# A perceiver layer on one core: the relative tables of self attention by column halves, and who makes four turning copies and two table copies

## The chip, the core and the metric

The kernel runs on one core of one Trainium2 chip. The core has a matrix engine (TensorE, PE in the profile, with PEld for its weight loads), VectorE (DVE), ScalarE (ACT), GpSimd (POOL) and SyncE (SP), which issues most transfers. The metric is the device time of one execution in microseconds (us). Before the change it is 780.18 us, the median of three runs from 779.72 to 780.61.

## What is computed

The layer has three parts, each added to its input: a cross attention of 128 positions to a context of 2048, a self attention with learned relative positions, and a gated attention that stands where a feed-forward block would. There are 4 sequences, 128 positions, width 512 and 16 heads of 32. All is in float32. The change is in the second part:

```python
r = jnp.arange(S)
rel = jnp.clip(r[:, None] - r[None, :], -MAX_DIST, MAX_DIST) + MAX_DIST
...
q, k, v = (proj(Wq), proj(Wk), proj(Wv))
a_q = Eq[rel]
a_k = Ek[rel]
a_v = Ev[rel]
content = jnp.einsum('bhld,bhmd->bhlm', q, k)
rel_k = jnp.einsum('bhld,lmd->bhlm', q, a_k)
rel_q = jnp.einsum('bhmd,lmd->bhlm', k, a_q)
pos_pos = jnp.einsum('lmd,lmd->lm', a_q, a_k)
logits = (content + rel_k + rel_q + pos_pos) * scale
attn = jax.nn.softmax(logits, axis=-1)
out = jnp.einsum('bhlm,bhmd->bhld', attn, v) + jnp.einsum('bhlm,lmd->bhld', attn, a_v)
```

For one position `l`, `rel_k` is the product of a window of the table (128 distances x 32) with the queries of that position in all 64 pairs of a sequence and a head. The kernel makes it so: 128 small products for `rel_k`, and 128 for `rel_q`.

## The kernel before

The cross attention takes the first three quarters of the time. It works through 16 blocks of 128 context positions in an order written out by hand. After it come the self attention (from about 600 us) and the gated attention (from about 695 us). In all three, each engine works through its instructions in the order in which the code issues them (`manual_schedule`), and waits on semaphores where a tile is not yet there or not yet free.

The stretch that the change touches stands at lines 799 to 887:

- `queries(c)` and `keys(c)`, for four chunks `c` of 128 columns: a projection on TensorE (`project_T`, line 215, 4 calls of 128x128 by 512) into a bank of the pool `bank`, and a copy to `qT` or `kT` by ACT (lines 868 and 873).
- `spread(src, n, half)`, after each second chunk: sixteen copies of 32x256 (line 811) that turn a part of `qT` or `kT` to the layout of `z`. In `z`, the four groups `g` of 32 partitions hold 32 positions each, and for each position the 64 pairs lie side by side. All of these "turning copies" are made by VectorE. `z[:, 0]` holds the queries, `z[:, 1]` the keys.
- `relative_k(n)` for `n` = 0 to 3, then `relative_q(n)` for `n` = 0 to 3: eight blocks. In each, `by_position` issues 32 matmuls (line 825), for eight positions and in turn for the four groups `g`. Each takes 32 rows of the table's window as weights, 128 columns wide, and 64 moving columns of `z`. Group `g` stands on its own 32 rows of the array and writes its own PSUM bank. A float32 matmul shows twice in the trace, with two weight loads.
- Blocks with even `n` write the four banks `psl` (tiles `s_rk`, `s_lg`), blocks with odd `n` two banks `pst` and two of the shared pool (tiles `s_rk` and `ps_rk`, `s_lg` and `ps_lg`). A block so waits for the copies of the block two before it, across the two tables.
- The first table's blocks are copied to `rk` (line 848): for `n` = 0 and 1 all four banks by ACT, for `n` = 2 and 3 banks 0 and 2 by ACT and 1 and 3 by VectorE.
- The second table's blocks go to `lg` with the positions' term `pos`: banks 0 and 2 by VectorE, which adds `pos` (line 863); banks 1 and 3 by ACT (line 860), and then GpSimd adds `pos` in SBUF (line 861). In the last block VectorE takes all four.

Then come the softmax's steps, again in an order by hand (lines 1065 to 1076): TensorE transposes parts of `rk` into PSUM (line 916) and adds the scores (line 931), VectorE joins them with `lg` (line 942) and takes maxima (line 948), ACT makes the exponentials (line 953). A join reads all positions of its heads, so it waits for all blocks and for GpSimd's additions. The tile `ev_win`, a load of 2 MB, takes the place of `z` and waits for the last product.

`by_columns` (lines 204 to 210) is an older helper, used in the cross attention: it issues one matmul as four, by 32 columns of the weights, each on its own column group.

## Time and profile before

| what | value |
|---|---|
| median of three runs | 780.18 us |
| the profiled execution, its time | 780.48 us |
| its span | 778.7 us |
| granted TensorE clock in it | 0.995 |
| the stretch 627.8 to 643.5 us: TensorE busy | 15.5 of 15.7 us |
| the same stretch: VectorE busy | 12.6 us |
| the same stretch: ACT busy | 10.7 us |
| the same stretch: GpSimd busy | 4.8 us |
| moved by DMA in it | 1 to 2% of the 16 engines' time |

The span runs from the first to the last instruction of one execution; the time of that execution is 1.8 us longer. The stretch is the one in which the eight blocks run. Its busy times are those of the profile's table by windows, two windows added. Further on, from 655 to 680 us, ACT is busy for 24.05 of 25 us with the exponentials.

In the profile a line such as `L825 PE MATMUL s_rk<-z,tabk 32*128 32x64` names the source line, the engine, the operation, the tile written and the tiles read, the weights' rows and columns, and the moving operand's partitions and columns. A helper's line stands for all of its callers.

### The profile page before, as it was taken

Reading aid. Unit: us, or ns where it says so; the run is one execution under the profiler, and the core shown is the slowest. Engines: PE = TensorE matmul, PEld = TensorE weight load, DVE = VectorE, ACT = ScalarE, POOL = GpSimd, SP = SyncE. Lnnn points to the kernel's source line nnn. Section 1 sums busy time; section 2 is a strip of 40 time slices with the busy share of each in tenths; the row PEclk is TensorE's granted clock in tenths of the full one; section 3 lists DMA queues with packets and bytes.
Section 4 is the critical chain, followed back from the end, with each engine's and each line's share of the span. In section 5 each row is a group of like instructions: output and inputs, shape, how many; then the busy total and the mean of one; then the engine's idle time right before and its main releaser. Section 6 shows DMA issues by size and latency. Waiting matters only on the chain.

```text
span 778.7 us, 28614 instructions
## 1 busy us (share of the span) xinstructions
PE 758.0 (97%) x13027; PEld 476.1 (61%) x13027; DVE 625.0 (80%) x642; ACT 527.6 (68%) x921; POOL 460.3 (59%) x296
## 2 busy tenths in 40 slices
PE   9999999999999999999999999997899999999998
PEld 5446566666666666666666666665253487674574
DVE  2158499999999999999999999998883689746463
ACT  2347777878788787887878878776813157923770
POOL 1623787859577595876958769599860015410261
PEclk9999999999999999999999999998999999999999
DMA  9310101101011010110101101033200005103001
GB/s 304 117 55 7 56 3 57 56 3 58 3 57 57 3 56 3 57 56 3 58 3 56 56 4 56 3 111 90 76 3 1 1 3 218 56 8 106 0 3 54
DMA packets 12619, 38.43 MB, mean 49 GB/s; under 512 B 1249, under 2 KB 1650, under 8 KB 10450
## 3 DMA queue, kind: packets, MB, share of 16 engines
q1 hardware_dynamic: 10802, 33.50, 12.5%
q8 instruction: 102, 1.67, 0.8%
q10 hardware_dynamic: 1248, 2.23, 0.8%
q0 software_dynamic: 448, 0.87, 0.5%
q14 instruction: 19, 0.16, 0.1%
HBM read 34.50 MB, written 2.10 MB: 47 GB/s over the span
## 4 chain that ended last, share of the span: by engine, by line
PE 88%; ACT 5%; DVE 5%; issue 1%; DMA 0%; POOL 0%; DVEq 0%; POOLq 0%; ACTq 0%
PE k L208 20%; PE ps_vu L208 12%; PE ps_s L458 9%; PE ps_vf L208 6%; PE ps_o L536 6%; PE ps_q L215 4%; PE ps_kc L208 3%; PE ps_vc L208 3%; PE ps_v L208 3%; ACT lg L953 2%; PE s_y L1367 2%; PE s_k L215 2%; PE out L208 2%; PE ps_k L215 2%; PE ps_k L556 2%; PE ps_sum L208 2%
## 5 line engine op out<-in xcount | busy, mean ns | idle before, releaser
L495 DVE TENSOR_TENSOR sg<-sg,stat 128x2048 f32<-128x2048 f32 x123 | 277.6, 2281 | 1.3 <-ACT rz L622 0.7
L470 ACT COPY sg<-ps_s 128x1024 f32<-128x1024 f32 x128 | 128.3, 1016 | 37.0 <-PE ps_s L458 21.5
L479 DVE TENSOR_TENSOR mx<-mx,ps_s 128x1024 f32<-128x1024 f32 x96 | 117.2, 1221 | 35.1 <-PE ps_s L458 22.6
L510 POOL TENSOR_TENSOR sm<-sm,sg 128x1024 f32<-128x1024 f32 x45 | 107.6, 2390 | 38.7 <-ACT sg L504 36.4
L504 ACT ACTIVATE sg<-sg 128x2048 f32<-128x2048 f32 x64 | 122.8, 1919 | 4.4 <-DVE sg L495 2.8
L511 POOL TENSOR_TENSOR sm<-sm,sg 128x1024 f32<-128x1024 f32 x45 | 107.5, 2389 | 3.5
L508 POOL TENSOR_TENSOR sm<-sg 128x1024 f32<-128x1024 f32 x16 | 38.4, 2398 | 93.8 <-ACT sg L504 93.8
L208 PE MATMUL k<-s,wk_sums 128*32 128x256 f32 x1440 | 86.7, 381 | 0.0
L458 PE MATMUL ps_s<-qT,kT 32*128 32x128 f32 x2048 | 76.8, 285 | 5.2 <-DVE mx L477 4.0
L458 PEld LDWEIGHTS ps_s<-qT,kT 32*128 32x128 f32 x2048 | 64.3, 188 | 24.6 <-issue 17.0
L208 PEld LDWEIGHTS k<-s,wk_sums 128*32 128x32 f32 x1440 | 43.9, 110 | 29.3 <-POOL s L311 0.2
L536 PE MATMUL ps_o<-sg,v 128*32 128x128 f32 x1792 | 60.1, 276 | 0.1
L536 PEld LDWEIGHTS ps_o<-sg,v 128*32 128x32 f32 x1792 | 51.9, 112 | 10.4 <-issue 1.3
L208 PE MATMUL ps_vu<-wv_sums,s 128*32 128x256 f32 x896 | 53.5, 379 | 0.0
L609 ACT COPY acc<-ps_o 128x512 f32<-128x512 f32 x56 | 32.9, 588 | 25.9 <-PE ps_o L536 24.7
L861 POOL TENSOR_TENSOR lg<-lg,pos 128x512 f32<-128x512 f32 x6 | 7.4, 1311 | 61.5 <-DVE lg L863 61.5
L208 PEld LDWEIGHTS ps_vu<-wv_sums,s 128*32 128x32 f32 x896 | 29.0, 110 | 19.2
L311 POOL TENSOR_TENSOR s<-ct,s 128x512 f32<-128x512 f32 x30 | 39.0, 1301 | 1.3
L311 POOL TENSOR_TENSOR s<-ct 128x512 f32<-128x512 f32 x30 | 38.6, 1287 | 0.2 <-PE ps_vu L208 0.2
L1265 POOL TENSOR_TENSOR e<-e,rs 128x512 f32<-128x512 f32 x16 | 16.3, 1040 | 36.6 <-DVE rs L1264 36.6
L606 ACT COPY ps_o<-acc 128x512 f32<-128x512 f32 x52 | 31.0, 596 | 6.4 <-DVE v L443 5.6
L489 DVE TENSOR_REDUCE stat<-mx 128x128 f32<-128x1024 f32 x16 | 32.8, 2052 | 0.1
(275 smaller groups left out, 1433.6 us busy)
## 6 DMA issues: line engine op xcount, KB each, us to landing
ct<-in_ctxT SPq DMA_DIRECT2D x15, 1024.0 KB, 4.8
ev_win<-in_tabv SPq DMA_DIRECT2D x1, 2048.0 KB
w_xattn_Wk<-in_xattn_Wk ACTq DMA_DIRECT2D x4, 256.0 KB, 6.5
ct<-in_ctxT SPq DMA_DIRECT2D x4, 256.0 KB, 6.4
x<-in_x SPq DMA_DIRECT2D x4, 256.0 KB, 8.6
w_xattn_Wv<-in_xattn_Wv ACTq DMA_DIRECT2D x1, 1024.0 KB, 12.4
w_xattn_Wq<-in_xattn_Wq SPq DMA_DIRECT2D x1, 1024.0 KB, 11.0
x_dram<-x SPq DMA_DIRECT2D x4, 256.0 KB, 2.4
```

The source lines that it names most:

```text
L208: nc.tensor.matmul(ps[cols], lhsT=lhsT[:, cols], rhs=rhs, start=start, stop=stop, skip_group_check=True)
L215: nc.tensor.matmul(ps, lhsT=w[:, k, c * P : (c + 1) * P], rhs=src[:, k, :], start=(k == 0), stop=(k == C - 1))
L311: nc.gpsimd.tensor_tensor(s_, x, y, op)
L458: nc.tensor.matmul(ps[i][:, cols], lhsT=kT[n, c // 2][rows, c % 2, cols], rhs=qT[rows, c, cols], start=(b == 0), stop=True, skip_group_che ...
L470: nc.scalar.copy(sg[n, c][:, k * HALF : (k + 1) * HALF], pss[n, c][k])
L479: nc.vector.tensor_tensor(mxs[n], mxs[n], pss[n, c][k], ALU.max)
L495: nc.vector.tensor_tensor(g, g, stat[:, row, :].unsqueeze(1).to_broadcast([P, NH * B, T]), op)
L504: nc.scalar.activation(sg[n, c], sg[n, c], AF.Exp, scale=SCALE)
L508: eng.tensor_tensor(t, g[:, 0:HALF], g[:, HALF:], ALU.add)
L510: eng.tensor_tensor(t, t, g[:, 0:HALF], ALU.add)
L511: eng.tensor_tensor(t, t, g[:, HALF:], ALU.add)
L536: nc.tensor.matmul(ps[i * HD : (i + 1) * HD, b * T : (b + 1) * T], lhsT=v[n, b // 2][:, b % 2, h * HD : (h + 1) * HD], rhs=sg[n, c][:, f * ...
```

## The change

A second helper issues a matmul as two, each with 64 columns of the weights, on its own half of the columns of the array and of the partitions of the PSUM bank. The tables' products use it: a block issues 64 matmuls instead of 32. Of the last group of turning copies (the keys' second half) those from the last 32 partitions of `kT`, one for each `g`, go to ACT. Of the first table's second block (`n` = 1), banks 1 and 3 are copied by VectorE instead of ACT.

```diff
+    def by_halves(ps, lhsT, rhs, start):
+
+        for i in range(2):
+            cols = slice(i * P // 2, (i + 1) * P // 2)
+            nc.tensor.matmul(ps[cols], lhsT=lhsT[:, cols], rhs=rhs, start=start, stop=True, skip_group_check=True)
...
-        def spread(src, n, half):
+        def spread(src, n, half, shared=False):
...
-                    nc.vector.tensor_copy(to[:, i, :, cs], from_[:, g])
+                    (nc.scalar.copy if shared and i == NH - 1 else nc.vector.tensor_copy)(to[:, i, :, cs], from_[:, g])
...
-                    nc.tensor.matmul(
-                        banks_of[g][:, j * NF : (j + 1) * NF],
-                        lhsT=tab[rows, s : s + T],
-                        rhs=z[rows, n, j0 + j, :],
-                        start=True,
-                        stop=True,
-                    )
+                    by_halves(banks_of[g][:, j * NF : (j + 1) * NF], tab[rows, s : s + T], z[rows, n, j0 + j, :], True)
...
-                copy = nc.vector.tensor_copy if n >= 2 and g % 2 else nc.scalar.copy
+                copy = nc.vector.tensor_copy if n >= 1 and g % 2 else nc.scalar.copy
...
             if c % 2:
-                spread(kT, 1, c // 2)
+                spread(kT, 1, c // 2, c == C - 1)
```

On TensorE, 256 matmuls of this stage become 512, so 512 entries of the trace become 1,024, with as many weight loads. On VectorE, 4 copies leave and 2 come. On ACT, 4 copies come, ahead of all copies of `rk`, and 2 leave. No transfer, no tile and no order between the engines' other instructions is changed.

## The prediction

> **What bounds the kernel now.** I read the page first, then the chain of waits for the stretch that the change touches, the rows by source line, and the timeline engine by engine.

> ```profile
> span 778.7 us, 28614 instructions
> PE 758.0 (97%) x13027; PEld 476.1 (61%) x13027; DVE 625.0 (80%) x642; ACT 527.6 (68%) x921; POOL 460.3 (59%) x296
> ```

> TensorE is busy for 97% of the span, but this average says little of one stage. The change touches only the relative tables, a stage of some 19 us, so the chain of waits (start, length, what) decides:

> ```profile
> 627.94 0.59 ACT kT L873
> 628.56 0.36 DVE z L811
> ...
> 634.37 0.38 DVE z L811
> 634.79 1.30 DVE rk L848 x2
> 636.13 1.90 PE s_lg L825 x59
> ...
> 643.49 1.90 PE s_l L916 x16
> ```

> Until 634.8 the end is set by VectorE's sixteen turning copies, then by two of its copies of the first table (`rk`), which free PSUM banks, and from 636 to 643.5 by the second table's products on TensorE (L825). So the stage has two limits in turn, and the diff touches both.

> What a product costs, by source line (least, median, greatest duration in ns):

> ```profile
> L825 PEld LDWEIGHTS s_rk<-z,tabk x192: 181/187/187, 627.8 to 635.4; 32*128 32x128 f32 x192
> L825 PE MATMUL s_rk<-z,tabk x192: 270/270/319, 627.8 to 635.5; 32*128 32x64 f32 x192
> ...
> L536 PEld LDWEIGHTS pso<-sg,v x128: 106/110/110, 571.1 to 582.9; 128*32 128x32 f32 x128
> L536 PE MATMUL pso<-sg,v x128: 272/273/297, 571.2 to 583.0; 128*32 128x128 f32 x128
> ```

> And the timeline (start, length, engine, line):

> ```profile
> 628.56 6.19 DVE L811 COPY z<-kT 32x256 f32<-32x256 f32 x16 [0.72 <-ACT kT L873]
> 634.79 1.89 DVE L848 COPY rk<-s_rk 128x512 f32<-128x512 f32 x3
> ...
> 629.91 3.03 ACT L848 COPY rk<-s_rk 128x512 f32<-128x512 f32 x6 [1.38 <-PE s_rk L825]
> ...
> 638.71 7.45 POOL L861 TENSOR_TENSOR lg<-lg,pos 128x512 f32<-128x512 f32 x6 [61.45 <-DVE lg L863]
> ...
> 629.89 0.28 PE L825 MATMUL s_rk<-z,tabk 32*128 32x64 f32 x2
> 629.91 0.28 PE L825 MATMUL ps_rk<-z,tabk 32*128 32x64 f32 x2
> 630.01 0.28 PE L825 MATMUL s_rk<-z,tabk 32*128 32x64 f32 x2
> ```

> A set of four (one per row group) starts within 0.02 us, and the next set comes 0.11 us later. GpSimd's six additions run without a gap from 638.71 to 646.16. The first join (L942) starts at 646.59, when the scores are done on TensorE.

> **The change, part by part.**

> *Products by halves.* Each of the 256 calls at L825 shows twice in the trace (two passes): 512 matmuls. A block is one relative_k or relative_q, 64 matmuls; 16 sets at 0.111 us make 1.78 us, and eight blocks 14.2 us. What is the 0.111? A load of 128 columns takes 187 ns and one of 32 takes 110, so a column costs 77/96 = 0.80 ns and 128 cost 103 ns: nearly the whole period. The 64 moving columns cost less: L208's rows of 256 and 512 columns (379 and 592 ns) give 0.83 ns a column, 53 ns. The set is bound by its weight load. A half loads 64 columns, 51 ns, so if two column groups load side by side a set of eight takes about 0.056 us, a block 0.9. Do they? L536 loads four column groups of 26 ns each. Loaded one behind the other, the first matmul after an idle stretch would lengthen by some 80 to 105 ns on the last group; the greatest there is 297 against a median of 273, +24. So they load side by side.

> What no row shows is the supply: twice as many pairs of load and matmul (1,024) at twice to four times the rate. Lower bound: four starts within 0.02 us, 7 ns a pair, eight in 56 ns, just enough. Upper bound: the fastest sustained row, L536, 32 in 0.88 us, 27.5 ns, so a block of 128 pairs takes 3.5 us. I take 7, because L536's 27.5 is explained by its own streaming (128 columns x 0.83 = 106 ns for four) and so says nothing of a limit on supply. The cost per block therefore lies between 0.9 and 3.5 us, taken 0.9; it is even with today's at 14 ns a pair.

> [...]

> *Four turning copies to ACT.* VectorE's last group shrinks from 16 to 12: 4 x 0.387 = 1.55 us, free at 633.2 instead of 634.75. ACT gets four copies of 32x256 ahead of its rk copies. No ACT row has this strided form. Its 128x512 PSUM copies follow each other at 0.49 us (six in 3.03, the last 0.58 long); an element costs (1016 - 588)/512 = 0.84 ns (L470 against L609), so 256 fewer make 0.28. The upper end is PE's strided row L1048 (four in about 0.15 us against L825's stream of 0.053), a factor 2.7: 0.75. I take 0.33, near the contiguous end: VectorE's copies of the same form follow each other at 0.387, little over half of the 0.6 of its 512-element copies, so the stride costs it little. ACT then ends its kT copy at 628.53, its turning copies at 629.85, and starts on block 0 when it does today (629.91), as the faster products have long arrived. At 0.75 it would finish 1.7 us later, at 633.6, about when VectorE becomes free; nothing is lost up to some 0.7 us a copy.

> *Half of block 1's rk copies to VectorE.* ACT loses two copies (0.98 us), VectorE gains two (1.2 us at 0.6). Behind them wait block 2's VectorE copies; for these wait the products of the second table.

> *The new order, step by step.* Blocks 0 and 1 on TensorE end at 628.7 and 629.6. ACT copies block 0 until 631.95; block 2 (same banks) runs until 632.9. VectorE ends turning at 633.2, copies two tiles of block 1 until 634.5 and two of block 2 until 635.7. Block 3 needs block 1's banks: 634.5 to 635.4. The second table's first block needs block 2's banks: 635.7 to 636.6. ACT's first lg copy ends at about 637.4 and GpSimd starts at 637.55, today 638.71: 1.2 us sooner. The remaining blocks alternate with copies (two a block on each engine, 1.25 us) and end at 640.2, 3 us sooner than today; transposes and scores end at 643.5 instead of 646.4.

> But the join needs GpSimd's additions too: 637.55 + 7.45 = 645.0. GpSimd takes TensorE's place as the last wait, 0.43 us of slack today. The join starts at 645.05 instead of 646.59: 1.5 us gained. Exponentials follow: ACT starts at 648.57 today, is nearly without gaps until 672, and moves along; it also loses its 0.2 us wait for the `v` copy at 655.17. Later weights (`ev_win`, ffn) start 3 us sooner, hidden either way. TensorE's 512 additional loads have no other place.

> **Sum.** 1.5 + 0.2 = 1.7 us off the span of 778.7: 777.0. The run profiled took 780.48, 1.8 above its span; the median of the three is 780.18. So 778.5. Within this likeliest case, 11 ns a pair (a block of 1.4 us) would give a gain of about 1.0, and GpSimd additions at the 1.04 us of L1265 in place of 1.24 would give 2.7: 777.5 to 779.2. What a measurement can tell from no change is 0.2%, 1.56 us; the bound is 778.62.

> **Rivals.**
> 1. *The product does not get faster* (the two halves of a row group load in turn, or supply is near 14 ns). Blocks stay at 1.8 to 1.9 us. VectorE is free sooner, but now has two copies more before block 3, at 634.5 instead of 634.0. Block 3 then ends at 636.3, the second table begins 0.3 us later and ends 0.2 to 0.5 later: 780.4. For it: no row has row and column groups together. Against it: L536's +24 ns.
> 2. *Supply of instructions, slower.* At 27.5 ns a pair a block takes 3.5 us, TensorE has no wait left, and eight blocks end at 627.84 + 28.2 = 656.0 instead of 643.4: 12.6 us later, 792.8. It decides from 14 ns a pair on; each ns above costs about 0.9 us. For it: no stretch of this trace sustains less than 27 ns. Against it: the fast starts, and that every such row is explained by its own columns.
> 3. *ACT's strided copies at 1 us or more.* Block 2 would start after 634.4, the second table at 637: the gain is eaten, 780.0 to 781.

> **Chances.** Forecast 0.62 (about three quarters of it beyond 0.2%), rival 1 0.17 (mostly no change), rival 2 0.15, rival 3 0.06 (half each). Faster 0.47, same 0.31, slower 0.22. The range 777.3 to 781.2 takes in the forecast, rivals 1 and 3; rival 2 and a little beside it lie outside.

> **What would show it.** After: loads of 64 columns at about 135 ns; a block's eight starts per 0.056 us, 16 such sets in 0.9 us; TensorE idle between the blocks; VectorE's last turning copies 12 in 4.7 us; GpSimd's additions starting near 637.5 and named as what released the first join. It is wrong if a block takes 1.8 us or more without waiting, if ACT's turning copies exceed 0.7 us, or if the joins begin sooner and the exponentials do not.

## The result and the profile after

The changed kernel takes 791.57 us, the median of four runs from 790.86 to 791.85; the kernel before takes 780.02 (four runs, 779.72 to 780.61). The ratio is 1.0144, with a 95% interval of 1.0132 to 1.0156: slower by 11.5 us, where 778.5 was forecast. The profiled execution took 790.86 us, its span is 789.1.

First the page, the engines and the row of the granted clock:

```profile
span 789.1 us, 29636 instructions
PE 760.1 (96%) x13539; PEld 477.1 (60%) x13539; DVE 625.2 (79%) x640; ACT 529.5 (67%) x923; POOL 460.8 (58%) x296
...
PEclk9999999999999999999999999998999959999999
```

TensorE is busy for 2.1 us more in a span that is 10.4 us longer: the rest is idle time. The 5 in the clock row is one slice of 20 us at about half clock. The rows by source line of the product (least, median, greatest ns) say that the tiles are as forecast where the clock is full, and that it isn't full for long:

```profile
L216 PEld LDWEIGHTS s_rk<-z,tabk x384: 127/131/227, 627.7 to 637.8; 32*64 32x64 f32 x192
...
L216 PEld LDWEIGHTS s_lg<-z,tabq x384: 173/222/228, 637.9 to 652.5; 32*64 32x64 f32 x192
```

A load of 64 columns takes 131 ns in the first table (forecast: about 135) and 222 in the second. The chain of waits through the second table:

```profile
630.98 2.06 ACT rk L848 x4
633.08 1.77 PE s_rk L216 x92
634.86 1.26 issue
...
638.37 1.22 issue
639.59 2.26 PE s_lg L216 x115
641.84 1.49 issue
...
645.58 1.49 issue
647.08 2.25 PE s_lg L216 x113
649.33 1.49 issue
```

After every run of matmuls TensorE stands still and waits for nothing that the profile shows ("issue"). Counted in the trace, these runs start at 636.12, 639.59, 643.33, 647.08 and 650.82, 3.47 to 3.75 us apart, and hold 128 pairs of load and matmul each (the last shows 121): 256 instructions. The queue that brings TensorE's instructions (q8) moves packets of 16 KB, 106 for the page's 27,078 matmuls and loads, 255 each. The change adds 1,024 instructions and 4 packets (102 to 106 in the whole execution), so a packet holds 256. From 627.6 to 653 it moved 7; before, 3 from 627.8 to 643.5 (packets, MB, share of the DMA engines' time):

```profile
q8 instruction: 7, 0.11, 1.9%
...
q8 instruction: 3, 0.05, 1.2%
```

A packet starts 1.04 to 1.14 us after each of these runs does (637.16, 640.69, 644.45, 648.22, 651.95), and the next run starts 2.4 to 2.6 us after the packet. My estimate from these times is a round trip, one packet at a time; what sets a packet off the trace doesn't show. The first two blocks, 256 pairs, ran from 627.65 to 630.44, 10.9 ns a pair.

The table by windows (window, its length, busy time of PE, PEld, DVE, ACT and POOL with their instructions, clock, DMA share, GB/s):

```profile
627.28:630.69 3.41, 3.38 (x258) 2.86 (x256) 2.62 (x7) 2.86 (x5) 0.00 (x0) 1.00 0.02 5
630.69:634.11 3.42, 2.02 (x110) 1.61 (x113) 3.31 (x8) 3.30 (x7) 0.00 (x0) 1.00 0.02 5
634.11:637.52 3.41, 2.15 (x144) 1.97 (x135) 1.50 (x3) 1.07 (x2) 0.00 (x0) 0.50 0.02 5
```

TensorE is busy for 2 of 3.4 us in the second window, and at its end the clock falls to 0.50; it comes back at 654.59. Two things are new, then: gaps in the supply and half a clock. The other engines wait for TensorE:

```profile
628.38 2.57 ACT L817 COPY z<-kT 32x256 f32<-32x256 f32 x4
...
642.42 2.49 POOL L861 TENSOR_TENSOR lg<-lg,pos 128x512 f32<-128x512 f32 x2 [65.30 <-DVE lg L863]
...
656.91 1.29 DVE L942 TENSOR_TENSOR lg<-s_l,lg 128x512 f32<-128x512 f32 x2 [1.54 <-PE s_l L931]
```

ACT's turning copies take 0.64 us each. GpSimd starts at 642.42 (before: 638.71), the joins at 656.91 (before: 646.59). These 10.3 us are, but for 0.1, the whole growth of the span.

### The profile page after: what moved, and what is told of

Read it like the earlier page. It is cut to its first block, busy times and chain, and to the rows that moved or that the text cites. A ratio compares the mean times of both kernels' runs of the same rounds, so it can differ in the third digit from the quotient of the medians.

```text
span 789.1 us, 29636 instructions
## 1 busy us (share of the span) xinstructions
PE 760.1 (96%) x13539; PEld 477.1 (60%) x13539; DVE 625.2 (79%) x640; ACT 529.5 (67%) x923; POOL 460.8 (58%) x296
## 4 chain that ended last, share of the span: by engine, by line
PE 88%; ACT 6%; DVE 4%; issue 2%; DMA 0%; POOL 0%; DVEq 0%; POOLq 0%; ACTq 0%
PE k L208 20%; PE ps_vu L208 11%; PE ps_s L464 9%; PE ps_vf L208 6%; PE ps_o L542 6%; PE ps_q L221 4%; PE ps_kc L208 3%; PE ps_vc L208 3%; PE ps_v L208 3%; ACT lg L953 2%; PE s_y L1367 2%; PE s_k L221 2%; PE out L208 2%; PE ps_k L221 2%; PE ps_k L562 2%
## 5 line engine op out<-in xcount | busy, mean ns | idle before, releaser
L208 PE MATMUL k<-s,wk_sums 128*32 128x256 f32 x1440 | 86.7, 381 | 0.0
L208 PEld LDWEIGHTS k<-s,wk_sums 128*32 128x32 f32 x1440 | 43.9, 110 | 29.3 <-POOL s L317 0.2
L542 PEld LDWEIGHTS ps_o<-sg,v 128*32 128x32 f32 x1792 | 51.8, 111 | 10.4 <-issue 1.3
L208 PE MATMUL ps_vu<-wv_sums,s 128*32 128x256 f32 x896 | 53.5, 379 | 0.0
L861 POOL TENSOR_TENSOR lg<-lg,pos 128x512 f32<-128x512 f32 x6 | 7.5, 1281 | 67.8 <-DVE lg L863 65.3
L208 PEld LDWEIGHTS ps_vu<-wv_sums,s 128*32 128x32 f32 x896 | 29.0, 110 | 19.2
L1265 POOL TENSOR_TENSOR e<-e,rs 128x512 f32<-128x512 f32 x16 | 16.3, 1041 | 36.6 <-DVE rs L1264 36.6
```

What stands on the lines that cost most here:

```text
L208: nc.tensor.matmul(ps[cols], lhsT=lhsT[:, cols], rhs=rhs, start=start, stop=stop, skip_group_check=True)
L542: nc.tensor.matmul(ps[i * HD : (i + 1) * HD, b * T : (b + 1) * T], lhsT=v[n, b // 2][:, b % 2, h * HD : (h + 1) * HD], rhs=sg[n, c][:, f * ...
```

## The experiments

Two theories stood first: too slow a supply of instructions (theory 1), and the halved clock (theory 2). Theory 3 blames the moved copies, theory 4 the tiles on row and column groups together.

**copies_only** and **halves_only**: each half of the change alone.

```diff
# copies_only: the change, but
-                    by_halves(banks_of[g][:, j * NF : (j + 1) * NF], tab[rows, s : s + T], z[rows, n, j0 + j, :], True)
+                    nc.tensor.matmul(banks_of[g][:, j * NF : (j + 1) * NF], lhsT=tab[rows, s : s + T], ...)
# halves_only: the change, but
-                copy = nc.vector.tensor_copy if n >= 1 and g % 2 else nc.scalar.copy
+                copy = nc.vector.tensor_copy if n >= 2 and g % 2 else nc.scalar.copy
-                spread(kT, 1, c // 2, c == C - 1)
+                spread(kT, 1, c // 2)
```

> The two moves of copies without the halves. Theory 1 (the instruction stream of TensorE is refilled too slowly for the 512 added pairs of load and matmul; one 16 KB packet per 3.5 to 3.75 us): the moves matter little. VectorE's twelve turning copies end at 633.0, ACT's first rk copies start at 631.0 instead of 629.9, block 2 runs from 632.9 and the second table's products start within 0.5 us of 636.1: 780.3, between 779.5 and 781.2. Theory 3 (the copies moved to ACT, at 0.64 us each, start the loss): 786 or more.

> The halves without the moves of copies. Theory 1: the whole loss is here, 789.5 to 792.5, with gaps of 1.2 to 1.8 us that wait for nothing but issue after every 128 pairs. Theory 3: under 781.

Measured: copies_only 792.31 us (ratio 1.0158, 1.0143 to 1.0173), halves_only 791.52 in one run. Each alone costs as much as both together. So theory 1, with its 780.3 for the copies, was only half of it. In copies_only the table products wait 0.8 us for issue in all (7.9 after the change), and TensorE is busy for 33.8 of the 34 us from 626; the same full-width products take longer. Its rows by source line:

```profile
L831 PEld LDWEIGHTS s_lg<-z,tabq x192: 328/328/328, 639.6 to 653.0; 32*128 32x128 f32 x192
L831 PE MATMUL s_lg<-z,tabq x192: 416/416/416, 639.7 to 653.1; 32*128 32x64 f32 x192
```

328 and 416 ns, where the kernel before has 187 and 270. The clock is at 0.50 from 632.35 to 656.24, after a window in which TensorE was busy for 3.23 of 3.41 us:

```profile
628.94:632.35 3.41, 3.23 (x101) 2.95 (x96) 3.30 (x9) 3.35 (x7) 0.00 (x0) 1.00 0.02 5
632.35:635.76 3.41, 3.41 (x52) 3.35 (x56) 2.05 (x5) 1.80 (x4) 0.00 (x0) 0.50 0.00 0
```

The stretches at half clock in these traces are multiples of 3.413 us, but for the last of each, which the end of the execution cuts short: 20.48 us after the change (six), 23.89 here (seven), and 6.83 (two) from 532.0 in the kernel before. So I laid windows of 3.41 us from the changes of the clock, which come at 632.35 here and at 634.11 after the change. I counted from the starts in the trace how much of the array each window used (moving columns x 0.83 ns, doubled at half clock, by the share of rows and columns of the tile; a few per cent of the records are missing):

```
kernel          window from   clock   array used   clock after
before             630.98      1.00      0.40         1.00
copies_only        628.94      1.00      0.36         0.50
after              630.69      1.00      0.21         0.50
halves_only        631.85      1.00      0.25         0.50
two_positions      630.20      1.00      0.28         0.50
copies_only        635.76      0.50      0.50         0.50
two_positions      633.62      0.50      0.91         1.00
copies_only        652.83      0.50      0.77         1.00
```

For example 102 starts x 64 columns x 0.83 ns x 32/128 = 1.36 of 3.41 us is the 0.40 of the kernel before. By this count the clock fell after every window of this stage at 0.36 or less. At half clock it did not come back after 0.50, nor after 0.75 in a window of other products (from 533.36 in copies_only), and it did after 0.77 and 0.91. Full-width table products count 0.48 at most at full clock (64 x 0.83 of each set's 111 ns) and 0.50 at half clock. Theory A is my estimate from these few windows: this stage lies a little above the use at which the clock falls and, once fallen, doesn't climb out by itself.

**two_positions** has the halves, the moves and the tiles, but no more instructions than before. It leaves out the second position's own window, so its values are not the layer's.

```diff
+                    if j % 2 == 0:
+                        moving = z[rows, n, j0 + j : j0 + j + 2, :].rearrange("p j f -> p (j f)")
-                    by_halves(banks_of[g][:, j * NF : (j + 1) * NF], tab[rows, s : s + T], z[rows, n, j0 + j, :], True)
+                        by_halves(banks_of[g][:, j * NF : (j + 2) * NF], tab[rows, s : s + T], moving, True)
```

> The change, but each half multiplies the moving columns of two positions at once (128 columns) with the window of the first of the two, so the second position of each pair gets the wrong window; a block then issues as many matmuls as before the change, 32, still on row and column groups, with the same tiles written. Theory 1: no gaps from issue; a block takes 0.9 to 1.1 us where nothing else holds it up; 778.3 to 780.0. Theory 2 (the clock, which falls to 0.5 because TensorE has idle moments, is the cause and not the supply): TensorE has more idle moments here than in the changed kernel, so the clock falls as well and the time is 784 or more. Theory 4 (tiles on row and column groups together are slow by themselves): 785 or more.

Measured: 779.31 us, ratio 0.9988 (0.9978 to 0.9998). The gaps are gone (1.0 us of issue in all), and theory 4 with them. The clock does fall, at 633.62, but these products stream 128 columns and use 0.91 of the array in that window, and after it the clock is back. The chain of waits now shows the forecast's order, with GpSimd last:

```profile
637.29 0.70 DVE lg L865
...
638.06 7.43 POOL lg L863 x6
```

So even without the supply limit the faster product is worth 0.1%: GpSimd's 7.4 us take over, as the forecast said, but from 638.06 instead of 637.55. The first join, at 645.52, waited 2.08 us for them.

**tiny_pairs** was meant to add instructions without work.

```diff
+                    nc.tensor.matmul(banks_of[g][0:1, j * NF : j * NF + 1], lhsT=tab[rows, s : s + 1],
+                        rhs=z[rows, n, j0 + j, 0:1], start=True, stop=True, skip_group_check=True)
```

> The kernel before, with one more matmul ahead of each table product: one weight column and one moving column, written where the product then overwrites it. That adds 512 pairs of load and matmul, as many as the halves add, with next to no work for the array. Theory 1: the same packets must be brought in, so the same loss: 788 to 793, with gaps from issue. Theories 2 and 4: the array's work is as before, TensorE is not idle and no new tile form streams 64 columns: 780 to 784.

Measured: 951.08 us, outside all theories. It tells nothing of the supply, since TensorE no longer runs side by side here. The timeline:

```profile
640.15 0.68 PE L834 MATMUL s_rk<-z,tabk 32*128 32x64 f32 x2
640.76 0.18 PE L826 MATMUL s_rk<-z,tabk 32*1 32x1 f32 x2
640.88 0.68 PE L834 MATMUL s_rk<-z,tabk 32*128 32x64 f32 x2
```

One position of one group takes 0.72 us, with the clock at 0.50. Whether the cause is the change of tile form on the same rows or the overwriting of the same PSUM element was not tried.

**copies_fill** and **halves_fill** raise the use of the array by work that nobody needs.

```diff
# copies_fill: copies_only, and in relative_k
+            if n == 2:
+                nc.tensor.matmul(ps[0], lhsT=ident, rhs=qT[:, 0, :], start=True, stop=True)
# halves_fill: the change, and in relative_k and relative_q, for each n
+            nc.tensor.matmul(ps[0], lhsT=ident, rhs=qT[:, 0, :], start=True, stop=True)
```

> The two moves of copies without the halves, and one matmul more, whose result is overwritten: 128x128 weights by 512 columns, put ahead of block 2's products, where TensorE waits for ACT in copies_only. It adds 0.86 us of work and takes nothing away. Theory A (the clock decides copies_only: where the array is used for less than some 0.38 of a window of 3.41 us, the clock falls to half, and the table products, at 0.5 at most, can't bring it back): the window that held 0.36 now holds about 0.6, the clock stays at 1.00, and the kernel takes 779.5 to 781.5, 11 us less than without the added matmul. Theory B (the copies themselves hold up TensorE): 792 or more.

> The changed kernel with the same added matmul ahead of each of the eight blocks: 8 x 0.86 = 6.9 us more work, which keeps the array's use above 0.45 even where a block comes only every 3.6 us. Theory 1 (supply: one packet of 256 instructions per 3.5 to 3.75 us, whatever the clock): the clock stays at 1.00, the gaps stay, and the added work falls into them: 789 to 793. Theory 2 (the clock alone made the changed kernel slow): no gaps; a block takes 1.4 + 0.86 = 2.3 us, eight end near 646: 782 to 784.

Measured: copies_fill 780.85 us (1.0012, 1.0002 to 1.0021). One added matmul makes copies_only 11.5 us faster. The clock stays at 1.00 through the windows in which it fell in copies_only, and the rows by source line are those of the kernel before again:

```profile
632.10:635.51 3.41, 3.41 (x100) 2.84 (x98) 2.72 (x7) 2.51 (x6) 0.00 (x0) 1.00 0.00 0
...
L831 PEld LDWEIGHTS s_lg<-z,tabq x192: 186/187/187, 636.3 to 643.4; 32*128 32x128 f32 x192
L831 PE MATMUL s_lg<-z,tabq x192: 270/270/270, 636.4 to 643.4; 32*128 32x64 f32 x192
```

halves_fill took 791.44 in one run, as long as the changed kernel though it has 6.9 us more of work, and at full clock, as its windows and its chain of waits show:

```profile
637.27:640.68 3.41, 2.03 (x116) 1.39 (x98) 1.26 (x2) 1.07 (x2) 0.00 (x0) 1.00 0.02 5
640.68:644.09 3.41, 2.70 (x131) 1.92 (x130) 1.41 (x3) 0.98 (x2) 0.72 (x1) 1.00 0.02 5
...
638.49 1.38 issue
...
642.62 0.71 issue
```

TensorE is idle for a good part of each window, and after each gap it starts at 636.39, 639.86, 643.33, 647.35, 650.82 and 654.29: 3.47 us apart, once 4.02. The supply takes as long at full clock (3.47) as at half (3.47 to 3.75). Both theories hold, each for its half of the change; in the two together the supply alone is enough for the whole loss. Three of its windows count 0.37 to 0.43 of the array, less than the 0.45 expected, and yet the clock held.

**halves_twice** puts a price on a packet.

```diff
                     by_halves(banks_of[g][:, j * NF : (j + 1) * NF], tab[rows, s : s + T], z[rows, n, j0 + j, :], True)
+                    by_halves(banks_of[g][:, j * NF : (j + 1) * NF], tab[rows, s : s + T], z[rows, n, j0 + j, :], True)
```

> The changed kernel with every half issued twice, the second overwriting the first with the same values: eight packets of instructions more (1,024 pairs), 11 us more of array work at full clock. Theory 1 (one packet per 3.5 to 3.75 us): 28 to 30 us more than the changed kernel, 819 to 822. If the array at half clock set the pace (15.3 ns a pair): 16 us more, about 807.

Measured: 821.34 us in one run, 29.8 more than the changed kernel for eight packets (114 instead of 106): 3.7 us each.

**act_turns** and **vector_rk**: which of the two moves brings the clock down?

```diff
# act_turns: the kernel before, with spread as the change has it, but
-                spread(kT, 1, c // 2)
+                spread(kT, 1, c // 2, c == C - 1)
# vector_rk: the kernel before, but
-                copy = nc.vector.tensor_copy if n >= 2 and g % 2 else nc.scalar.copy
+                copy = nc.vector.tensor_copy if n >= 1 and g % 2 else nc.scalar.copy
```

> The kernel before with only the four turning copies given to ACT. ACT starts on block 0's copies at 631.0 instead of 629.9, TensorE waits from about 631.4 to 633 for them, and again for block 1's. Theory A: a window of 3.41 us at or under about 0.37 of the array, the clock at 0.50 to the end of the stage: 790 to 794. If the waits alone counted: 780.5 to 782.

> The kernel before with only the second block's copies shared with VectorE. ACT's copies of block 0 start at 629.9 as before, but block 3 now waits for VectorE, which turns until 634.8 and then copies until 636: TensorE idle for some 2 us before 636. Theory A: the clock falls there and stays at 0.50: 790 to 795. If the waits alone counted: 781.5 to 782.5.

Measured, one run each: 792.02 and 789.40. Each does it alone. The clock fell at 633.52 (seven windows) and at 636.54 (five), after windows that count 0.26 and 0.20 of the array. The windows of vector_rk:

```profile
633.13:636.54 3.41, 1.80 (x52) 1.67 (x56) 3.14 (x6) 0.89 (x2) 0.00 (x0) 1.00 0.00 0
636.54:639.95 3.41, 3.41 (x72) 3.41 (x72) 1.29 (x2) 1.07 (x2) 0.00 (x0) 0.50 0.02 5
```

789.40 is 0.6 us under the expected span of times; two windows less at half clock go with it.

**gpsimd_turns** gives the four copies to GpSimd instead.

```diff
-                    nc.vector.tensor_copy(to[:, i, :, cs], from_[:, g])
+                    eng = nc.gpsimd if shared and i == NH - 1 else nc.vector
+                    eng.tensor_copy(to[:, i, :, cs], from_[:, g])
...
-                spread(kT, 1, c // 2)
+                spread(kT, 1, c // 2, c == C - 1)
```

> The kernel before, with the four turning copies that the change gives to ACT made by GpSimd, which has nothing to do until 638.7; the copies of the first table as before. ACT starts on block 0 at 629.9 as before, so TensorE waits no longer than before and the clock stays at 1.00 by theory A. VectorE is free at 633.0 to 633.3, the second table starts at 635.5 to 635.8 instead of 636.1: 779.2 to 780.0. By theory B (the turning copies of VectorE set the pace and any engine that takes some of them brings the whole) 778.5 or less.

Measured: 780.17 us, 1.0007 (0.9998 to 1.0016): no gain, and just over the 779.2 to 780.0 expected. The clock stayed at 1.00 in this stage, as theory A said (the execution's mean is 0.996, before 0.995), but the timeline shows where the relief went:

```profile
628.28 5.98 DVE L812 COPY z<-kT 32x256 f32<-32x256 f32 x12 [0.73 <-ACT kT L874]
...
628.39 2.95 POOL L812 COPY z<-kT 32x256 f32<-32x256 f32 x4 [51.14 <-ACT kT L874]
```

VectorE's twelve copies take 5.98 us beside GpSimd's four, and 4.62 beside ACT's. VectorE is free at 634.3 instead of 633.

**dip_filled** and **dips_filled** use the lesson elsewhere, in the kernel before. The windows there:

```profile
528.58:531.99 3.41, 0.84 (x20) 0.38 (x8) 2.64 (x2) 2.94 (x3) 3.41 (x2) 1.00 0.78 225
531.99:535.41 3.42, 0.84 (x16) 0.84 (x20) 2.11 (x3) 3.39 (x7) 3.42 (x2) 0.50 0.21 82
535.41:538.82 3.41, 3.41 (x64) 3.02 (x64) 3.13 (x2) 1.67 (x2) 2.33 (x2) 0.50 0.02 5
```

After a wait of 3.96 us for VectorE's maxima TensorE works a full window at half clock (535.41).

```diff
# in scores(n, c)
+            if (n, c) == (NK - 1, 1):
+                for _ in range(4):
+                    nc.tensor.matmul(ps[0], lhsT=ident, rhs=qT[:, c, :], start=True, stop=True)
# dips_filled has this too, in sum_up
+                for _ in range(2):
+                    nc.tensor.matmul(late["sum"], lhsT=ident, rhs=wo[:, 0, :], start=True, stop=True)
```

> The kernel before with four added matmuls (128x128 by 512 columns, 3.4 us, results overwritten) at another place, ahead of the second chunk's scores of the last block of the cross attention. There TensorE waits from 528.9 to 534.6 and the clock is at 0.5 for two windows (532.0 to 538.8) in the kernel before. Theory A: the clock stays at 1.00, and the 4.2 us of work that ran at half clock run up to 2 us shorter: 778.0 to 779.5. If the clock there costs nothing because VectorE sets the pace: 780.

> dip_filled with two more matmuls ahead of the sums (ps_sum), where TensorE waited from 553.4 to 555.4 for ACT and the clock fell for one window (556.0 to 559.4) in that run. Theory A: no fall before the tables in any execution, and 0.5 to 1.5 us less than dip_filled where it fell: 777.3 to 778.6, a ratio of 0.996 to 0.9985 to the kernel before. If the pace there is set elsewhere: the same as dip_filled, 778.8.

Measured: dip_filled 778.80 us (0.9985, 0.9972 to 0.9998), in two groups that the mean clock tells apart: five executions at 1.000 took 777.28 to 777.71, five at 0.997 or 0.998 took 779.90 to 780.65. In the profiled one of the second group the clock fell for the one window from 555.95. In the first group the mean clock of 1.000 leaves no room for that; why it held there, whether by how the windows lie or not, isn't shown, since no trace of them is at hand. dips_filled fills that place as well: 777.85 us, 0.9972 (0.9961 to 0.9982), and the page's clock row has no dip left:

```profile
PEclk9999999999999999999999999999999999999999
```

It beats both kernels, the changed one and the one before (780.42, measured together with it), though by estimate it has 6 x 0.86 = 5.2 us more of work for TensorE (one of halves_fill's added matmuls took 0.86). There is no stretch at half clock in its profile before the last instructions.

## Why the prediction was wrong

- **Supply of instructions: the step that failed.** "I take 7, because L536's 27.5 is explained by its own streaming (128 columns x 0.83 = 106 ns for four) and so says nothing of a limit on supply." The streaming does explain L536, but that a row is explained by one limit doesn't exclude another at the same height. The runs showed a burst of 256 pairs at 10.9 ns, and then 128 pairs per 3.5 to 3.75 us, 27 to 29 ns a pair, a block of 3.5 us or more where 0.9 was taken. Rival 2 had this size (27.5 ns, a block of 3.5 us, 792.8 against 791.57) and got 0.15. Part of its nearness is luck: it took the figure from L536's streaming, and it had all eight blocks at 3.5 us and the products end at 656.0, where the first two blocks took 2.8 us together and the products ended near 653. What could have raised its chance was in the trace: the queue of instruction packets, whose closest packets in the kernel before lie 3.68 us apart, and 3.72 and 3.79 in this very stage. At 64 matmuls a block that stage needs a packet every 3.56 us by count; the change doubled the need.
- **ACT's turning copies.** Taken at 0.33 us, measured 0.64, inside the bounds of 0.28 to 0.75. That "nothing is lost up to some 0.7 us a copy" is the second step that failed: with full-width products, act_turns lost 11.6 us at that price (one run), because TensorE's waits for ACT left 0.26 of the array in use in the window after which the clock fell.
- **The clock.** No step had a term for it; every duration was taken at the granted 0.995. "TensorE idle between the blocks" was listed as a sign of success, and it was the danger. The trace of the kernel before had an example: after a window in which TensorE was busy for 0.84 of 3.41 us (from 528.58) the clock was at 0.50 for 6.83 us. Nor was TensorE idle wherever it fell: in copies_only it was busy for 3.23 of 3.41 us in the window after which the clock fell, with 0.36 of the array in use.
- **What was right.** Loads side by side (131 ns a load, forecast about 135), VectorE's twelve copies (4.62 us, forecast 4.7), and GpSimd as the last wait once TensorE is faster (two_positions). The sets of eight were right at their best alone: the fastest follow each other at 58 ns (forecast 56), but the first two blocks' mean is 87, the 11 ns a pair that the prediction had as a less favourable case. Rival 3 had the right place, but its condition (1 us a copy) did not come true, and it was priced at 780 to 781, without the clock.
- **Why the two losses don't add.** At half clock a block of halves takes 1.94 us (636.12 to 638.06), and the next packet is there only after 3.5 to 3.75. The slower clock hides in the gaps. That is why 791.57, 792.31 and 791.52 look like one cause and are two.

## What to carry to other kernels

## What was not expected of the hardware

- The table stage of copies_only stayed at half clock though TensorE was busy without a pause (1.00 of each us from 633 to 656): 0.50 of the array over five full windows did not bring the clock back, nor did 0.64 in act_turns (from 650.59) and 0.75 in copies_only (from 533.36). It came back after 0.77 (copies_only), 0.87 (the kernel before, from 535.41) and 0.91 (two_positions).
- The falls follow the count less closely. Windows counted at 0.37 fell in one execution (dip_filled) and held in others (halves_fill, vector_rk, and the kernel before from 685.59). Products of 512 columns are counted badly by their starts: the window from 553.84 in copies_only counts 0.28 and held, but 0.36 to 0.40 if each product is spread over the time that it streams. The levels come from traces with a few records missing, and whether the clock's control counts as I do stays open.
- VectorE's SBUF copies took 0.50 us each beside GpSimd's and 0.39 beside ACT's (5.98/12 and 4.62/12).
- A one-column matmul ahead of each product, on the same rows and the same PSUM element, cost 171 us in 256 products, most of them at half clock.
